# Layer 0 cross attention of a two-layer transformer: queries by seven block products for twelve of sixteen elements, the total of the sums formed earlier, and a weight folding of the second FFN moved

## The chip, the cores and the metric

The kernel runs on one core of a Trainium2 chip. The metric is the device time of one execution in microseconds (us). Three executions of the kernel before took 2147.99, 2148.72 and 2149.63 us; their median, 2148.72, is the time before. One further execution was profiled.

Engines are called as in the profile: PE multiplies matrices (PEld is its loading of the stationary operand), DVE, ACT and POOL are the vector, scalar and GpSimd engines, SP issues most DMAs. PE writes to PSUM, eight banks of 512 fp32 per partition; POOL reads and writes SBUF alone.

## The reference

Sixteen elements x[b] of 256 tokens by 256 features go through two layers, in fp32. Each layer is self attention, cross attention to a context of 256 tokens by 192 features, and an FFN, with residuals:

```
h = layernorm(x) * (1 + scale(cond)) + shift(cond)
q = h @ wq ; k, v = split(ctx_n @ wkv)          # layer 0: 16 heads of 64, rotary on q and k
x = x + softmax(q k^T / 8) v @ wo + bo
h2 = layernorm(x) ...                            # FFN: x = x + gelu(h2 @ w1 + b1) @ w2 + b2
```

In layer 0 wq is 256 x 1024, so the queries of one element are a 256 x 256 by 256 x 1024 product. The queries of the cross attention of layer 0 are what most of the change concerns. The second FFN is that of layer 1.

## The kernel before, in words

The work is a list of jobs: phase p (0: self of layer 0, 1: cross of layer 0, 2: FFN, 3 to 5: the same for layer 1) times element b. An attention job has two steps, s = 0 and 1, of two units each; a unit is four heads. The order of the instructions on each engine is the order of the code (a manual schedule); an instruction waits in its engine's queue until what it needs has happened, and whatever stands behind it waits too. A tile pool with a given number of buffers makes a writer wait for the last reader of the buffer that it takes over.

In step (b, s) of a layer 0 attention the code emits, for the probabilities of the units 2s and 2s + 1 (whose scores were formed at the end of the step before): on DVE the sum of the two halves of the probabilities (`stage_t`, tile both), its transposition in blocks (`stage_turn`, tile squares) and a reduction (`stage_reduce`, tile rows); on PE the products with the values (`layer0_sums`, L817), copied to SBUF by ACT (tile raw). In between it prepares the next step: queries and keys (`rotary`, `stage_rotary`). There PE forms q and k of one half unit side by side in one bank, DVE multiplies the bank by cosines and sines (tiles m, L707, 128 x 512), and POOL combines two such tiles (tile qk, L715, 128 x 512). At the end of the step PE forms the scores of the next step's two units (`scores`, `stage_s`, L750) in the eight banks, and ACT takes the exponential (L763).

Each product is cut in four strips of 32 output partitions that run side by side in the array (`product`, L84); one fp32 matmul shows as two records in the trace.

The tail of an element: when its four units are reduced, `sum_up` lets PE add the rows across partitions (the total), DVE takes the reciprocal, SP writes it to DRAM (sums_seen) and reads it back spread over 32 partitions each (tile spread), and POOL multiplies the four raw tiles by it (`scale`, L806). POOL then forms sums of blocks (`fold_inner`, L1099: 5, 2, 1 in step 0 and 7, 6 in step 1), and PE multiplies them by folded blocks of wo, seven products in place of eight (`finish_folded`), after which DVE adds them to x. In the kernel before, all of this for element b - 1 lies in element b's steps: the total in step 0 after the first rotations, the products at the end of step 1.

In step 0 PE also forms the values of the next element (`layer0_values`), and DVE the moments of the element three ahead and of its context; in step 1 DVE normalizes both, SP turns them through DRAM (turned, fetched), and ACT and POOL apply the modulation (tile hT).

The self phase (p = 0) already forms queries by seven block products for the elements 3 to 15: with wq and h cut into 2 x 2 blocks, seven products of sums of blocks take the place of eight products of blocks. `fold_query_weights` forms the sums of the weights once, `fold_tokens` those of h for each element (both on POOL), `query_part` issues the products in seven parts, with copies by ACT (tiles kept) and two additions by DVE on the way, `keys` forms the keys apart, and `rotate` turns queries and keys in separate tiles (L612 and L618 on DVE, L627 on POOL, 128 x 256 each on POOL).

In an FFN the elements from 2 on go in pairs (`pair_hidden`, again seven products). At the border between the elements 1 and 2 of layer 1's FFN, DVE folds the inputs of the pair (`fold_input`, L935 to L938), then the blocks of w2 (`fold_output_weights`, L1009 to L1012), then takes moments, and then adds the first of pair_hidden's sums (L968), which PE waits for before it may write that bank again.

## Time and profile before

| | us |
|---|---|
| median of three executions | 2148.72 |
| profiled execution, timed | 2152.08 |
| its span in the profile | 2150.3 |
| PE busy | 2136.8 |
| DVE busy | 1676.3 |
| POOL busy | 1340.8 |
| ACT busy | 905.9 |
| one cross element of layer 0 (809 to 847 us) | 38.42 |
| one self element of layer 0 with queries by seven (334 to 374 us) | 39.66 |

A timeline row reads: start and duration in us, engine, line, operation, output<-inputs, shapes, how many instructions were merged, and in brackets the time that the engine stood idle before it and what ended that. A row of the table by stretches gives the length, then the busy time of PE, weight loads, DVE, ACT and POOL (in parentheses how many instructions), then the clock granted to PE as a share of full speed, the share of DMA and GB/s.

### The profile page before, as it was taken

Reading aid. Unit: us, or ns where it says so; the run is one execution under the profiler, and the core shown is the slowest. Engines: PE = TensorE matmul, PEld = TensorE weight load, DVE = VectorE, ACT = ScalarE, POOL = GpSimd, SP = SyncE. Lnnn points to the kernel's source line nnn. Section 1 sums busy time; section 2 is a strip of 40 time slices with the busy share of each in tenths; the row PEclk is TensorE's granted clock in tenths of the full one; section 3 lists DMA queues with packets and bytes.
Section 4 is the critical chain, followed back from the end, with each engine's and each line's share of the span. In section 5 each row is a group of like instructions: output and inputs, shape, how many; then the busy total and the mean of one; then the engine's idle time right before and its main releaser. Section 6 shows DMA issues by size and latency. Waiting matters only on the chain.

```text
span 2150.3 us, 112524 instructions
## 1 busy us (share of the span) xinstructions
PE 2136.8 (99%) x51248; PEld 1442.3 (67%) x51248; DVE 1676.3 (78%) x3060; ACT 905.9 (42%) x1455; POOL 1340.8 (62%) x1346
## 2 busy tenths in 40 slices
PE   9999999999999999999999999999999999999998
PEld 5666767767766666666666658886666655656887
DVE  5878888888888888888888867865777777777765
ACT  3333334333342333333333334433666666664442
POOL 4888778778768777776777756662322233235773
PEclk9999999999999999999999999999999999999999
DMA  6110110110132311212212033221212232223321
GB/s 196 29 39 23 29 38 23 29 38 23 40 109 59 90 45 39 63 35 48 55 41 58 23 80 88 56 49 23 63 39 43 51 98 62 61 49 78 76 64 40
DMA packets 307039, 117.83 MB, mean 55 GB/s; under 512 B 243364, under 2 KB 289784, under 8 KB 306424
## 3 DMA queue, kind: packets, MB, share of 16 engines
q1 hardware_dynamic: 305320, 108.71, 20.7%
q8 instruction: 403, 6.60, 1.3%
q10 hardware_dynamic: 1232, 1.84, 0.3%
q14 instruction: 84, 0.69, 0.1%
HBM read 77.14 MB, written 33.29 MB: 51 GB/s over the span
## 4 chain that ended last, share of the span: by engine, by line
PE 85%; DVE 3%; POOL 3%; issue 1%; DMA 1%; SPq 0%; ACT 0%; DVEq 0%; POOLq 0%; ACTq 0%
PE banks L84 54%; PE banks L750 15%; PE banks L817 9%; PE banks L836 5%; PE banks L686 2%; PE banks L503 1%; POOL raw L806 1%; POOL folded L1099 1%; POOL qk L627 0%; DMA spread<-sums_seen 0%; POOL qk L715 0%; DVE x L1053 0%; DVE bn L351 0%; POOL rstd L357 0%; SPq L797 0%
## 5 line engine op out<-in xcount | busy, mean ns | idle before, releaser
L763 ACT ACTIVATE pr<-banks 128x1024 f32<-128x1024 f32 x576 | 487.4, 937 | 434.1 <-PE banks L750 319.9
L715 POOL TENSOR_TENSOR qk<-m,m 128x512 f32<-128x512 f32 x152 | 221.4, 1478 | 123.8 <-DVE m L707 119.0
L769 DVE TENSOR_TENSOR both<-pr 128x1024 f32<-128x1024 f32 x128 | 177.8, 1389 | 86.1 <-ACT pr L763 84.6
L750 PE MATMUL banks<-qk 32*64 32x256 f32 x8192 | 240.9, 378 | 1.0 <-POOL qk L715 0.5
L817 PE MATMUL banks<-pr,v 128*32 128x256 f32 x4096 | 241.2, 379 | 0.0
L750 PEld LDWEIGHTS banks<-qk 32*64 32x64 f32 x8192 | 184.7, 131 | 61.3 <-issue 16.8
L827 ACT COPY raw<-banks 128x512 f32<-128x512 f32 x128 | 75.1, 587 | 331.4 <-PE banks L817 327.5
L707 DVE TENSOR_TENSOR m<-banks,rope 128x512 f32<-128x512 f32 x304 | 189.7, 679 | 22.5 <-POOL qk L715 13.4
L627 POOL TENSOR_TENSOR qk<-m,m 128x256 f32<-128x256 f32 x208 | 168.0, 832 | 61.9 <-DVE m L618 38.6
L817 PEld LDWEIGHTS banks<-pr,v 128*32 128x32 f32 x4096 | 132.4, 110 | 94.1 <-issue 17.3
L806 POOL TENSOR_TENSOR raw<-raw,spread 128x512 f32<-128x512 f32 x128 | 162.1, 1296 | 22.9 <-DMA spread<-sums_seen 22.5
L453 POOL TENSOR_TENSOR x<-x,bo_b 128x256 f32<-128x256 f32 x96 | 73.3, 783 | 162.5 <-DVE xh L365 162.5
L878 POOL TENSOR_TENSOR oT<-oT,spread 128x256 f32<-128x256 f32 x64 | 45.8, 736 | 205.2 <-DVE spread L877 205.2
L775 DVE STREAM_TRANSPOSE squares<-both 128x1024 f32<-128x1024 f32 x128 | 158.0, 1235 | 1.8
L782 DVE TENSOR_REDUCE rows<-squares 128x32 f32<-128x1024 f32 x128 | 155.0, 1211 | 1.3
L1099 POOL TENSOR_TENSOR folded<-raw,raw 128x512 f32<-128x512 f32 x90 | 141.5, 1600 | 2.4
L836 PE MATMUL banks<-pr,wide_v 128*32 128x256 f32 x2048 | 134.3, 379 | 0.0
L84 PE MATMUL banks<-hT,wq_ca 128*32 128x256 f32 x2048 | 134.0, 379 | 0.0
L750 PE MATMUL banks<-q,k 32*64 32x256 f32 x4096 | 128.2, 381 | 0.0
L84 PE MATMUL banks<-hT,wk_sa 128*32 128x256 f32 x2048 | 126.5, 382 | 0.0
L1053 DVE TENSOR_TENSOR x<-banks,x 128x256 f32<-128x256 f32 (+2 forms) x150 | 79.6, 531 | 56.1 <-PE banks L84 49.8
L750 PEld LDWEIGHTS banks<-q,k 32*64 32x64 f32 x4096 | 87.4, 131 | 38.0 <-issue 13.9
(270 smaller groups left out, 4408.9 us busy)
## 6 DMA issues: line engine op xcount, KB each, us to landing
turned<-blocks SPq DMA_DIRECT2D x380, 64.0 KB
fetched<-turned SPq DMA_DIRECT2D x380, 64.0 KB
spread<-sums_seen SPq DMA_DIRECT2D x128, 128.0 KB
x<-in_x SPq DMA_DIRECT2D x16, 256.0 KB
fetched_c<-turned_c SPq DMA_DIRECT2D x64, 64.0 KB
cT<-in_ctx_turned SPq DMA_DIRECT2D x16, 256.0 KB
out<-x SPq DMA_DIRECT2D x15, 256.0 KB
ctx<-in_ctx SPq DMA_DIRECT2D x16, 192.0 KB
```

Source lines behind the costliest of these rows:

```text
L84: nc.tensor.matmul(out[cut], lhsT[:, cut], rhs, start=start, stop=stop, **more)
L627: nc.gpsimd.tensor_tensor(out, cos[i], sin[1 - i], (ALU.subtract, ALU.add)[i])
L707: nc.vector.tensor_tensor(m, pq, rope[:, s : s + 1, :].to_broadcast([P, 2, N]), ALU.mult)
L715: nc.gpsimd.tensor_tensor(r, x, y, (ALU.subtract, ALU.add)[out])
L750: nc.tensor.matmul(banks[64 * g : 64 * g + 64, at + h, t * N : (t + 1) * N], lhs, rhs, start=(half == 0 and (t == 0 or job["layer"] == 1)) ...
L763: nc.scalar.activation(pr[:, one], sc[:, one], AF.Exp, scale=0.125 if job["layer"] == 0 else 0.25)
L769: nc.vector.tensor_tensor(both, pr[:, :, 0, :], pr[:, :, 1, :], ALU.add)
L775: nc.vector.transpose(job["squares"].rearrange("p b k -> p (b k)"), job.pop("both").rearrange("p h n -> p (h n)"))
L806: nc.gpsimd.tensor_tensor(part, part, spread[:, u : u + 1, :].to_broadcast([P, 2, N]), ALU.mult)
L817: nc.tensor.matmul(o[32 * h : 32 * h + 32, half, :], v[:, t, col : col + 32], pr[:, h, t, :], start=(t == 0), stop=(t == NT - 1),)
L836: nc.tensor.matmul(o[32 * h : 32 * h + 32], v[:, t, 4 * c + h, 32 * e : 32 * e + 32], pr[:, h, t, :], start=(t == 0), stop=(t == NT - 1),)
L1099: eng.tensor_tensor(folded[m], *sums[m])
```

## The change

1. Cross phase of layer 0, elements 4 to 15: the queries are formed by seven block products, as in the self phase. The weights' sums are formed in step 1 of the elements 2 and 3, on POOL; the sums of h in step 0 of the element before, on POOL, one of them in place in hT. The keys' rotations come before the queries'. The banks differ: keys in the banks 0 and 1, queries in 2 and 3.
2. For these elements the total of the sums is formed in `finish_folded` of step 1, before the last of its seven products, in place of the following step 0. The write and the spread read are issued there too, ahead of the turned blocks. In step 0 POOL scales the first raw tile ahead of the rotations, the second after the keys' rotations, the others after the queries'.
3. Layer 1's FFN: `fold_output_weights` on DVE moves from step 3 of element 1 to step 0 of element 2, behind pair_hidden's first sum.
4. Small tiles share pools (flat with ctx, its turned blocks with blocks), bn has two buffers in place of four and inv32 one in place of two.

The diff, cut:

```diff
     def fold_tokens(job, eng):
         b = [[job["hT"][:, k, t * P : (t + 1) * P] for t in range(NT)] for k in range(KC)]
+        if job["cross"]:
+            few = work.tile([P, 3, P], F32, tag="tokens", name=f"tokens_{job['key']}", bufs=1)
+            t1, (t2, t3, t4) = b[0][1], (few[:, i] for i in range(3))
+            eng.tensor_tensor(t3, b[1][1], b[0][1], ALU.subtract)
+            eng.tensor_tensor(t1, b[0][1], b[0][0], ALU.subtract)
+            eng.tensor_tensor(t2, b[1][1], t1, ALU.subtract)
+            eng.tensor_tensor(t4, b[1][0], t2, ALU.subtract)
...
     def queries_by_seven(then):
-        return then is not None and then[0]["p"] == 0 and then[0]["b"] > 2
+        return then is not None and then[0]["layer"] == 0 and then[0]["b"] > (3 if then[0]["cross"] else 2)
...
+    def form_total(job, at):
+        product(bank(at, 32), job.pop("rows").rearrange("p u b -> p (u b)"), fold, True, True)
...
-    def finish_folded(job, at, between=None):
+    def finish_folded(job, at, between=None, total=None):
...
             for c in range(4):
                 product(places[m], hidden[m][:, c, :], weights[m][:, c, :], c == 0, c == 3)
+            if m == 7 and total:
+                form_total(total, 6)
...
+        if total:
+            sum_up(total, 6)
         nc.vector.tensor_tensor(outer, third[:, 0:1, :].to_broadcast([P, 2, P]), outer, ALU.add)
...
-            if b == 2 and s == 0 and layer0:
-                add()
+            if b == 2 and s == 0:
+                if layer0:
+                    add()
+                else:
+                    fold_output_weights(job["phase"], nc.vector)
...
                     fold_input(jobs[j + 1 : j + 3], nc.vector)
-                    if not layer0:
-                        fold_output_weights(job["phase"], nc.vector)
...
-            if queries_by_seven(then):
+            if queries_by_seven(then) and then[0]["cross"]:
+                early = s == 0 and "spread" in late
+                stage_t(job, 2 * s)
+                stage_turn(job, 2 * s)
+                for half in range(2):
+                    keys(then, 0, half)
+                query_part(then, 0)
+                for half in range(2):
+                    keys(then, 1, half)
+                stage_t(job, 2 * s + 1)
+                if early:
+                    scale(late, 0)
+                elif s == 0:
+                    sum_up(late, 6)
+                rotate(then, 0, 1)
+                if s == 1:
+                    fold_inner(late, nc.gpsimd, 7, 6)
+                rotate(then, 1, 1)
+                if early:
+                    scale(late, 1)
+                query_part(then, 1)
+                query_part(then, 2)
+                layer0_sums(job, 2 * s, 4, (0,))
+                query_part(then, 3)
+                layer0_sums(job, 2 * s, 4, (1,))
+                query_part(then, 4)
+                stage_reduce(job, 2 * s)
+                if s == 1:
+                    stage_turn(job, 3)
+                layer0_sums(job, 2 * s + 1, 5)
+                query_part(then, 5)
+                if s == 0 and queries_by_seven((nxt, 0)):
+                    fold_tokens(nxt, nc.gpsimd)
+                rotate(then, 0, 0)
+                query_part(then, 6)
+                rotate(then, 1, 0)
+                if s == 0:
+                    scale(late, *((2, 3) if early else range(4)))
+                    stage_turn(job, 1)
...
+                stage_reduce(job, 2 * s + 1)
+            elif queries_by_seven(then):
...
-                if then:
+                if then and then[0]["cross"]:
+                    finish_folded(late, (4, 5), total=job if queries_by_seven(then) else None)
+                elif then:
                     finish_folded(late, (4, 5), (lambda: stage_reduce(job, 3)) if queries_by_seven(then) else None)
```

## The prediction

> **What bounds the kernel now.** I read the page's busy times, then the idle times of each engine over the span, then the order of time of one cross element of layer 0, and last the same for a self element, which already forms its queries by seven block products.
>
> ```profile
> span 2150.3 us, 112524 instructions
> ...
> PE 2136.8 (99%) x51248; PEld 1442.3 (67%) x51248; DVE 1676.3 (78%) x3060; ACT 905.9 (42%) x1455; POOL 1340.8 (62%) x1346
> ```
>
> ```profile
> 814.95:833.78 18.83, 18.83 (x364) 10.00 (x360) 18.47 (x34) 5.68 (x8) 10.88 (x11) 1.00 0.37 88
> 833.78:853.37 19.59, 19.59 (x533) 14.55 (x529) 14.41 (x21) 7.26 (x11) 17.59 (x14) 1.00 0.04 10
> ```
>
> These two stretches are the halves (step 0, step 1) of one cross element, each from the start of its scores; after the span come PE, weight loads, DVE, ACT, POOL. PE has no gap: 18.83 + 19.59 = 38.42 us, and the following elements repeat it to 0.1 us. Time goes only if matmul work goes. DVE is next, 32.9 of 38.4 us.
>
> ```profile
> 820.09 1.05 PE L84 MATMUL banks<-hT,wq_ca 128*32 128x256 f32 x16
> 820.96 0.61 PE L84 MATMUL banks<-cT,wk_ca 128*32 128x256 f32 x8
> ```
>
> ```profile
> 366.48 0.62 PE L84 MATMUL banks<-hT,wq_sa 128*32 128x128 f32 x16
> 366.92 0.62 PE L84 MATMUL banks<-tokens,wq_sa 128*32 128x128 f32 x16
> 367.35 1.91 PE L84 MATMUL banks<-hT,wk_sa 128*32 128x256 f32 x32
> ```
>
> Starts count, not the durations, which overlap. 16 records of 256 columns, a quarter of a step's queries, take 0.87 us. A block product (16 records of 128 columns) takes 0.44, 0.43: half, so the shorter stream costs nothing extra.
>
> ```profile
> 1960.22 1.05 PE L84 MATMUL banks<-hT,w_b 128*32 128x256 f32 x16
> 1963.35 1.07 PE L84 MATMUL banks<-inner,input_w_L_xcond_b 128*32 128x256 f32 x16 [2.09 <-DVE sums L968]
> 1964.24 3.37 PE L84 MATMUL banks<-w_b,g 128*32 128x128 f32 x64
> ...
> 1978.07 1.93 PE L84 MATMUL banks<-w_b,g 128*32 128x128 f32 x64
> ```
>
> ```profile
> 1961.20:1963.40 2.20, 0.11 (x8) 0.05 (x7) 2.06 (x7) 0.84 (x2) 0.56 (x1) 1.00 0.40 90
> 1963.40:1965.50 2.10, 2.10 (x48) 1.76 (x52) 1.92 (x5) 1.05 (x2) 1.57 (x3) 0.77 0.81 219
> 1965.50:1967.40 1.90, 1.90 (x43) 1.90 (x39) 0.76 (x2) 0.96 (x3) 1.82 (x3) 0.50 1.00 372
> ```
>
> This is the longest PE wait of the kernel, in the second FFN: 2.09 us for DVE. After it the granted clock (the third figure from the end) falls to 0.77 and 0.50; 64 records that take 1.74 us later (1978.07 to 1979.81) take 3.12 (1964.24 to 1967.36).
>
> **Part 1: the queries.** Removed per step: four quarters of 0.865, 3.46 us. Added: seven block products of 16 records, 7 x 0.436 = 3.05 us. Gain 0.41 us a step; 12 elements x 2 steps: **-9.8 us**, if PE gets no new waits. The key products and what they wait for keep their number. The self phase shows that it need not: its elements take 39.66 us, PE busy 39.66. But the cross phase is fuller, so I lay out both steps, with T0 and T1 the starts of their scores. PE: 18.83 - 0.41 - 0.06 (the total moves) = 18.36 for step 0, 19.59 - 0.41 + 0.06 = 19.24 for step 1, together 37.60.
>
> ACT gains one copy within the bank and two "kept" copies (0.37 each): 2.2 us an element on an engine busy 12.9; PE needs each some 0.9 us after it is made. Nothing.
>
> DVE gains two adds of 0.42 a step, 1.7 us an element: 34.6 of 37.6. Its waits before show the room:
>
> ```profile
> 837.87 1.50 DVE L769 TENSOR_TENSOR both<-pr 128x1024 f32<-128x1024 f32 x1 [3.37 <-ACT pr L763]
> ```
>
> Step 1, from T1 + 4.1 (first exponentials done): two sums of probabilities with a transposition between 3.83, key rotations 2.40, add 0.42, reduction 1.2, transposition 1.25, both query rotations with the second add 2.87, reduction 1.15: T1 + 17.2. PE forms the total at T1 + 18.3, one product before the end: **1.1 us to spare**. This is the new wait; behind it on PE stands all that follows. Residual adds, reciprocal, norm and context norm then end by T0 + 3.9, when the next exponentials end at T0 + 4.1. Step 0 from T0 + 4.25: 7.7 us of the same work to T0 + 11.95, the query rotations (released by PE at 12.7) to 15.5, the rest to 20.8 = T1 + 2.4. In time.
>
> POOL turns each unit's two 512-wide rotations (2.52 us) into two pairs of 256-wide ones (2 x 1.43), +1.4 us an element, and gains four token sums: in the self rows 0.46, 1.42 (median), 0.46, 0.46, together 2.9 us with the gaps. Its order in step 0 is what matters: the first scaling now stands ahead of all rotations, and it waits for a DMA.
>
> ```profile
> 346.45 0.35 DVE L791 RECIPROCAL inv<-banks 128x32 f32<-128x32 f32 x1
> 354.52 2.53 POOL L806 TENSOR_TENSOR raw<-raw,spread 128x512 f32<-128x512 f32 x2 [0.28 <-DMA spread<-sums_seen]
> 1092.76 0.34 DVE L791 RECIPROCAL inv<-banks 128x32 f32<-128x32 f32 x1
> 1102.32 4.97 POOL L806 TENSOR_TENSOR raw<-raw,spread 128x512 f32<-128x512 f32 x4 [1.72 <-DMA spread<-sums_seen]
> ```
>
> ```profile
> 349.22 2.27 POOL L627 TENSOR_TENSOR qk<-m,m 128x256 f32<-128x256 f32 x2 [1.52 <-DVE m L618]
> 352.80 1.43 POOL L627 TENSOR_TENSOR qk<-m,m 128x256 f32<-128x256 f32 x2 [1.31 <-DVE m L618]
> ```
>
> From reciprocal to landing: 8.1 us (self), up to 9.6 (cross, behind the turned blocks and the context in SP's queue). The change puts sums and spread ahead of those, so I take 8.1. The reciprocal starts near T0 - 0.5: landing T0 + 7.6, scaling to 8.9, key pairs (DVE done at 9.1 and 10.3) to 12.0, scaling 13.2, tokens 16.1, query pairs 17.6 and 19.0. Scores want them at 18.36 and 20.2: **0.8 us to spare**; at 9.6 us latency 0.5 short (scaling to 10.4, and all behind it 1.3 later). On SP the turned writes wait for sums and spread, about 1.5 us later than now; their fetch was issued at T0 + 14.1 and is used at T1 + 14: hidden. The context follows them, at about T0 + 10 instead of 8.8, and is read at T0 + 18 or later: hidden. Tile renames and pool depths: DVE uses the moment tiles in order, nothing.
>
> The row for tokens was taken beside DVE's sums of probabilities. [...]
>
> The sums of the query weights (eight POOL adds of 0.83, two elements' step ends, a whole element before use): hidden; at elements 2 and 3 they could delay POOL once by 3 us, of which 0 to 1 shows. I take 0.3.
>
> **Part 2: second FFN.** Without four DVE sums (0.7, 0.6, 0.6, 0.6) the awaited sum ends at 1960.8 instead of 1963.3, before PE needs it (1961.09). PE gains 2.26 there. But the four now stand ahead of the norm (1.35) and of the next sum: 1960.8 + 2.5 + 1.35 + 0.65 = 1965.3, and PE, at full clock, comes to it at 1963.7: a new wait of 1.6 us. PE's product of 1967.36 starts at 1965.4: -2.0. With the clock up, the 0.29 that this product and the next lost to the half clock (1.16 for 0.87) is won too: -2.3. If the clock falls as it did after 2.09 us, 1.38 + 0.29 is lost again: -0.6. The nearer row is the wait of 2.09 (another, 0.52 at 1958.47, left the clock at 1.00), but the new one is shorter, so I take the middle, **-1.4**, and keep both ends.
>
> [...]
>
> **Sum.** -9.8 - 1.4 + 0.3, and 0.5 for two such waits of 0.25 us as scores have for POOL in the run before (1254.70: 0.28): -10.4 us. The profiled span goes from 2150.3 to 2139.9 (that execution was timed at 2152.08, 3.4 above the median); the median from 2148.72 to **2138.3**.
>
> **Rivals.** (a) Part of the gain is eaten: spread late as in the cross rows (9.6 us) or the total 0.4 us late costs 0.35 to 0.7 an element, 4 to 8 us: 2142.3 to 2146.3. For it: rooms of 0.8 and 1.1 us. Against: the shorter SP queue. (b) Slower: POOL is late in step 0. Each us behind shows once an element at the scores, and POOL's tail in step 1 then holds the rotation tiles, DVE's reduction and the total. The gain of 10.4 is gone at 0.87 us an element, and +0.2% is reached at 1.22; past the room of 0.8 that is POOL 1.7 and 2.0 us later than laid out, for instance 9.6 us latency (1.3) plus one stretched pair (0.84, the rows of 2.27 against 1.43). Some 2153 to 2160. (c) No change: weight loads, 128 columns apiece, become the limit and queries save nothing; only Part 2 remains, 2147.3. Against: 0.436 us a product in the self rows.
>
> **Chances.** Forecast (2135.5 to 2142) 0.66, (a) 0.16, (b) 0.11 slower and 0.03 around zero, (c) 0.04. The low end is -9.8 - 2.3 with no waits, less 1 us for the spread of runs; the range 2135.5 to 2146 holds the forecast and nearly all of (a), 0.81. A measurement tells 0.2% (4.3 us) from no change, at 2144.4, which splits (a) 0.09 to 0.07: faster 0.75, same 0.14, slower 0.11.
>
> **What would show it.** Right: cross elements 5 to 14 at 37.6 us with PE busy as long; query products of 0.436; PE waits on the POOL rotations and on the total under 0.2 us each; FFN wait of 2.09 gone, a shorter one some 2.5 us on. Wrong: PE or its weight loads waiting for the POOL query rotation at each step 1's scores, for the reduction ahead of the total, or the spread's DMA landing later than T0 + 8.5.

## The result and the profile after

The changed kernel takes 2143.04 us (median of 10 runs, 2141.77 to 2144.71); the kernel before, run beside it, 2148.60 (2144.99 to 2150.51). The ratio is 0.9975, with a 95% interval of 0.9965 to 0.9984: 5.6 us less. The forecast was 10.4 us less, 2138.3, with a range of 2135.5 to 2146. The direction is right and the time lies in the range, but about half of the gain is missing. Where it went is the subject of what follows.

The page of the changed kernel begins like that of before: PE is busy for 99% of the span.

```profile
span 2141.9 us, 115148 instructions
...
PE 2125.1 (99%) x52400; PEld 1472.1 (69%) x52400; DVE 1697.6 (79%) x3108; ACT 931.5 (43%) x1527; POOL 1375.6 (64%) x1498
```

The steady elements are as forecast. These are PE rows of the timeline of the changed kernel (start, time, engine, line, operation, out<-in, number of records): the scores of element 6's step 1 and of element 7's steps 0 and 1, with two of the block products in the first of these steps.

```profile
910.50 3.71 PE L768 MATMUL banks<-qk 32*64 32x256 f32 x128
...
922.55 0.62 PE L84 MATMUL banks<-tokens,wq_ca 128*32 128x128 f32 x16
922.99 0.62 PE L84 MATMUL banks<-hT,ms_of_query_weights_True 128*32 128x128 f32 x16
...
929.75 3.71 PE L768 MATMUL banks<-qk 32*64 32x256 f32 x128
...
948.10 3.71 PE L768 MATMUL banks<-qk 32*64 32x256 f32 x128
```

A block product starts 0.44 us after the one before it. The two steps take 19.25 and 18.35 us; the undisturbed elements take 37.56, where 38.42 stood before. That is 0.86 us an element, a little more than the 0.82 forecast.

The loss stands at the two ends of the run of elements. Here are the PE rows with the longest waits of that phase (the wait and its releaser in brackets), again of the changed kernel.

```profile
814.50 0.22 PE L84 MATMUL banks<-fold,rows 128*32 128x32 f32 x1 [0.99 <-DVE rows L800]
...
822.50 0.65 PE L84 MATMUL banks<-hT,wq_ca 128*32 128x128 f32 x16 [0.78 <-POOL wq_ca L559]
...
1245.98 0.66 PE L768 MATMUL banks<-qk 32*64 32x256 f32 x6 [1.83 <-POOL qk L643]
1246.91 5.38 PE L768 MATMUL banks<-qk 32*64 32x256 f32 x122 [0.27 <-DVE m L629]
```

The first two belong to elements 3 and 4, where the block products begin: PE waits for the total of the sums, which waits for DVE, and then for the sums of the query weights. The last two are the scores of element 15's step 1, for which POOL's rotations come late. They also take 5.4 us in place of 3.7. The windows from 1245.98 on say why: the third figure from the end is the granted clock.

```profile
1245.98:1247.98 2.00, 1.73 (x38) 1.08 (x46) 2.00 (x3) 0.00 (x0) 1.68 (x3) 0.91 0.68 251
1247.98:1249.98 2.00, 2.00 (x48) 1.59 (x40) 1.97 (x6) 0.01 (x1) 2.00 (x3) 0.50 0.14 44
1249.98:1251.98 2.00, 2.00 (x60) 1.43 (x46) 0.86 (x4) 1.93 (x2) 1.90 (x3) 0.73 0.04 8
```

In the second FFN the wait of 2.09 us is gone, and the new one stands 3 us later, ahead of the next product. It is 1.38 us long (1.6 were forecast), and the clock stays at 1.00.

```profile
1956.02 1.93 PE L84 MATMUL banks<-w_b,g 128*32 128x128 f32 x64
1959.33 1.07 PE L84 MATMUL banks<-inner,w_b 128*32 128x256 f32 x16 [1.38 <-DVE sums L1010]
```

One reading needs care. The two profiled spans differ by 8.4 us, the medians by 5.6. The profiled execution of before was one of the longer ones of its kernel, and the time from the start to element 3's scores, which the change leaves as it was and the later kernels nearly so, varies between 774.0 and 778.6 us over the thirteen profiles of this study. So the stages are compared one by one below, each by its own length.

### The profile page after: what moved, and what is told of

It is laid out like the page before. It is cut to its first block, busy times and chain, and to the rows that moved or that the text cites. A ratio compares the mean times of both kernels' runs of the same rounds, so it can differ in the third digit from the quotient of the medians.

```text
span 2141.9 us, 115148 instructions
## 1 busy us (share of the span) xinstructions
PE 2125.1 (99%) x52400; PEld 1472.1 (69%) x52400; DVE 1697.6 (79%) x3108; ACT 931.5 (43%) x1527; POOL 1375.6 (64%) x1498
## 3 DMA queue, kind: packets, MB, share of 16 engines
q10 hardware_dynamic: 1232, 1.84, 0.2%
## 4 chain that ended last, share of the span: by engine, by line
PE 85%; POOL 3%; DVE 3%; issue 1%; DMA 1%; SPq 0%; ACT 0%; DVEq 0%; POOLq 0%; ACTq 0%
PE banks L84 54%; PE banks L768 15%; PE banks L839 9%; PE banks L858 5%; PE banks L704 1%; PE banks L503 1%; POOL raw L828 1%; POOL folded L1121 1%; POOL qk L733 0%; DMA spread<-sums_seen 0%; DMA sums_seen<-inv 0%; DVE x L1075 0%; DVE m L629 0%; POOL qk L643 0%; DVE xh L365 0%
## 5 line engine op out<-in xcount | busy, mean ns | idle before, releaser
L643 POOL TENSOR_TENSOR qk<-m,m 128x256 f32<-128x256 f32 x400 | 303.9, 788 | 78.8 <-DVE m L636 47.2
L787 DVE TENSOR_TENSOR both<-pr 128x1024 f32<-128x1024 f32 x128 | 182.8, 1428 | 63.2 <-ACT pr L781 59.8
L828 POOL TENSOR_TENSOR raw<-raw,spread 128x512 f32<-128x512 f32 x128 | 168.5, 1337 | 50.8 <-DMA spread<-sums_seen 40.3
L629 DVE TENSOR_TENSOR m<-banks,rope 128x512 f32<-128x512 f32 x200 | 128.3, 683 | 21.7 <-PE banks L84 12.1
L636 DVE TENSOR_TENSOR m<-banks,rope 128x512 f32<-128x512 f32 x200 | 125.2, 676 | 1.7 <-POOL qk L643 0.8
L733 POOL TENSOR_TENSOR qk<-m,m 128x512 f32<-128x512 f32 x56 | 78.3, 1419 | 35.3 <-DVE m L725 32.4
```

What stands on the lines that cost most here:

```text
L629: nc.vector.tensor_tensor(view, bank(2 + e if job["cross"] else 2 * e).rearrange("p (t h n) -> p t h n", t=2, h=2), rope[:, i, :].rearrang ...
L643: nc.gpsimd.tensor_tensor(out, cos[i], sin[1 - i], (ALU.subtract, ALU.add)[i])
L787: nc.vector.tensor_tensor(both, pr[:, :, 0, :], pr[:, :, 1, :], ALU.add)
L828: nc.gpsimd.tensor_tensor(part, part, spread[:, u : u + 1, :].to_broadcast([P, 2, N]), ALU.mult)
```

## The experiments

### The kernel before, once more

Is the wait of 2.09 us with its fallen clock in every execution, or was the first profile an unlucky one?

> The kernel before, unchanged, profiled a second time. Theory A (the wait and the fallen clock in the second FFN belong to every execution): a PE wait of about 2.1 us for the DVE sums of the second FFN again, the granted clock at 0.77 and 0.50 after it, span near 2150. Theory B (the first profiled execution, timed 3.4 us above the median, was an unlucky one): the wait is 1 us or less, or the clock stays at 1.00 after it, and the span is 1.5 to 3.5 us shorter, 2146.5 to 2148.5. In both the steady cross elements take 38.4 us.

The wait is there again, 2.09 us to a hundredth, but the clock does not fall. These are the PE rows and two windows behind them.

```profile
1963.55 1.07 PE L84 MATMUL banks<-inner,input_w_L_xcond_b 128*32 128x256 f32 x16 [2.09 <-DVE sums L968]
1964.44 1.93 PE L84 MATMUL banks<-w_b,g 128*32 128x128 f32 x64
```

```profile
1964.60:1965.60 1.00, 1.00 (x48) 1.00 (x40) 1.00 (x3) 0.45 (x1) 1.00 (x2) 1.00 0.72 139
1965.60:1966.60 1.00, 1.00 (x37) 0.85 (x32) 0.85 (x2) 0.72 (x3) 1.00 (x2) 1.00 1.03 426
```

The 64 records take 1.93 us here; in the first profile of before they took 3.37. Each theory was right in one half: the wait belongs to the kernel, the clock does not. The span was 2150.1, no shorter, because of waits elsewhere (1.46 us for POOL at 601 us, in a stretch that the change does not touch).

### The second FFN alone

```diff
 (the kernel before)
-            if b == 2 and s == 0 and layer0:
-                add()
+            if b == 2 and s == 0:
+                if layer0:
+                    add()
+                else:
+                    fold_output_weights(job["phase"], nc.vector)
...
                     fold_input(jobs[j + 1 : j + 3], nc.vector)
-                    if not layer0:
-                        fold_output_weights(job["phase"], nc.vector)
```

> The kernel before with the second FFN's four weight sums moved, and nothing else. Theory A: the whole of what the two profiles show there, 2.1 + 0.3 us, so 2.2 to 2.6 us faster than before by the medians (2146.2 of 2148.6). Theory B: what is won is the shorter wait alone, or less, 0 to 1 us (2147.6 to 2148.6). The profile is to show the wait of 2.09 gone, one of 1.2 to 1.6 us for the later DVE sums about 1 us before the output products, and a clock of 1.00 there, by both.

Measured: 2147.90 against 2148.80 of before, ratio 0.9996 (0.9988 to 1.0005), that is 2.6 us less to 1.1 more. By the medians alone nothing can be said. The stretch itself is clearer. From the hidden products ahead of the wait to the last output products of the pair it takes 17.71, 16.37 and 16.31 us in the three profiles without the move (the first with the fallen clock), and 14.20 to 14.82, in the mean 14.47, in the ten with it. So the move is worth 1.9 us against the two profiles in which the 64 records behind the wait took 1.93 us, the clock up, and 3.2 against the one in which the clock fell to 0.50 and they took 3.37. The new wait was 0.98 us in this run and 1.04 to 1.38 in the others (mean of the ten 1.22). Two smaller waits are gone as well: one of 0.52 us for DVE ahead of the long one in the first profile, and one of 0.65 and 0.56 us behind it, for which the profile names no releaser, in the other two.

### The queries alone

```diff
 (the changed kernel)
-            if b == 2 and s == 0:
-                if layer0:
-                    add()
-                else:
-                    fold_output_weights(job["phase"], nc.vector)
+            if b == 2 and s == 0 and layer0:
+                add()
...
                     fold_input(jobs[j + 1 : j + 3], nc.vector)
+                    if not layer0:
+                        fold_output_weights(job["phase"], nc.vector)
```

> The changed kernel without the move in the second FFN: queries and total only. By both theories the steady elements take 37.56 us and the waits at the entry (elements 3 and 4) and at the last element stand as in the changed kernel. Theory A: 3.0 to 3.5 us faster than before by the medians (2145.3), that is the whole 5.6 less the FFN's 2.3. Theory B: 4.6 to 5.6 us faster (2143.0 to 2144.0).

Measured: 2143.53 against 2148.80, ratio 0.9979 (0.9969 to 0.9988), 5.3 us less, as the second theory had it, though the interval (2.6 to 6.7 us) holds the first as well. The profile repeats the waits of the changed kernel: 0.98 for the rows, 0.79 for the weight sums, 1.84 ahead of the last scores. This time the clock stayed up after the 1.84: the 122 records of those scores took 3.69 us, in place of 5.38.

With these profiles the queries' part can be read without the noise of the rest: from the scores of element 3's step 1 to those of element 15's step 1 the kernels with direct queries take 456.1, 455.8 and 456.1 us, those with block products 451.2, 451.4 and (in a later run) 452.1. At 37.56 an element without a wait it would be 445.4 (19.21 for element 3's step 1, eleven elements of 37.56, and 13.52 less 0.48 for the last step). So of 10.6 us, 4 to 5 arrive.

### Three edits at the two ends

```diff
 (the changed kernel)
-            if s == 1 and job["b"] in ((2, 3) if job["cross"] else (1, 2)):
-                weights_after = job["b"] - 2 if job["cross"] else job["b"] - 1
+            if job["cross"] and (job["b"], s) in ((2, 1), (3, 0)):
+                weights_after = job["b"] - 2
...
-        if layer0 and not ffn and s == 1 and job["b"] == 3:
+        if layer0 and not ffn and s == (0 if job["cross"] else 1) and job["b"] == 3:
             late_mod = phases[job["p"] + 1]
...
-                layer0_sums(job, 2 * s + 1, 5)
+                if not leaving:
+                    layer0_sums(job, 2 * s + 1, 5)
                 query_part(then, 5)
...
                 rotate(then, 1, 0)
+                if leaving:
+                    layer0_sums(job, 1, 5)
                 if s == 0:
-                    scale(late, *((2, 3) if early else range(4)))
+                    scale(late, *((1, 2, 3) if leaving else (2, 3) if early else range(4)))
...
```

> The changed kernel with three edits: the second half's weight sums formed one step sooner, the FFN's factors computed one step sooner (both at element 3), and in element 15's step 0 the last sums over values placed after the query products, with the second scaling after the query rotations. My theory: the queries' gain is lost at the two ends of the run of elements, 2.5 us at the entry and 3.0 to 3.4 at the last element. Then the waits there (0.99 for the DVE rows, 0.78 and 0.28 for the weight sums, 1.83 and 0.27 before the last scores) shrink below 0.3 each, the clock stays at 1.00 at the last scores, and the time is 4 to 5.5 us below the changed kernel's 2143.0, at 2137.5 to 2139. Rival: the waits are DVE's and POOL's load of work that has to be done anyway; they come up again a step later, and the time is within 1 us of 2143.0.

A miss: 2145.51 against 2148.80, ratio 0.9986 (0.9977 to 0.9994), less of a gain than the changed kernel's. The last element was mended: its step 0 took 13.77 us in place of 14.94, the wait of 1.83 was 0.32, and the clock stayed up: the 122 records of the scores took 3.69 us. But element 3's step 1 took 27.01 us in place of 20.78. The second half's weight sums, moved to the end of step 0, stand ahead of step 1's rotations on POOL. These are rows of POOL, DVE and PE from that step.

```profile
809.95 0.73 POOL L561 TENSOR_TENSOR ms_of_query_weights_True<-wq_ca,ms_of_query_weights_True 128x256 f32<-128x256 f32 x1
810.63 1.40 POOL L643 TENSOR_TENSOR qk<-m,m 128x256 f32<-128x256 f32 x2
```

```profile
812.07 1.29 DVE L629 TENSOR_TENSOR m<-banks,rope 128x512 f32<-128x512 f32 x2 [4.35 <-POOL qk L643]
...
815.89 1.29 DVE L629 TENSOR_TENSOR m<-banks,rope 128x512 f32<-128x512 f32 x2 [2.19 <-POOL qk L643]
817.10 1.21 DVE L800 TENSOR_REDUCE rows<-squares 128x32 f32<-128x1024 f32 x1
```

```profile
818.36 0.26 PE L84 MATMUL banks<-fold,rows 128*32 128x32 f32 x1 [3.91 <-DVE rows L800]
```

The chain reads upward: PE waits for the rows; DVE forms them right after its last query rotation; that rotation waited because the tiles `m`, two of each kind, were not free; POOL frees them when it has added the key rotations, and POOL was late. So 3.2 us of POOL work (four sums, 807.51 to 810.68) at the end of a step 0 cost 6.2 us against the changed kernel's first profile, and 5.2 against the kernel further below that leaves these sums in step 1 (21.79). This gave a new theory: the loss at the entry comes through these buffers, not through DVE's own work.

### The changed kernel again

> The changed kernel, unchanged, timed beside the others of this set. Both theories: 2141.5 to 2144.5 by the median; from the scores of element 3's step 1 to those of element 15's step 1 451.2 us (451.2 and 451.4 in the two profiles so far, against 456.1, 455.8 and 456.1 with the old queries). My theory of the clock, that after a wait of 1.8 to 2.1 us it falls in some executions and not in others: the wait of 1.83 before the last scores is there again, and the scores take 3.7 us (clock up) or 5.4 (clock down), either way.

2142.39 against 2148.93, ratio 0.9974 (0.9963 to 0.9985). The stretch takes 452.1 us. The wait for the rows at element 3 is 2.23 us here (0.99 in the first profile): DVE waited 2.24 us for POOL's buffers, against 1.13. The scores after the wait of 1.83 took 5.38 us, as in the first profile, with the clock down again.

### The three places, mended with less

The weight sums stay in step 1, only ahead of the norm and the inputs of later elements; the other two edits (the factors, and element 15's last sums and scaling) are as above.

```diff
 (the changed kernel, with the factors and element 15 as above)
             else:
+                if weights_after is not None and job["cross"]:
+                    fold_query_weights(job["phase"], weights_after, nc.gpsimd)
                 prepare_norm(third)
                 prepare_context(third)
...
```

> As the kernel with all three edits, but the second half's weight sums stay at the end of step 1 of element 3 and only go ahead of the norm and the input of later elements there; the factors one step sooner and the last sums after the query products as in that kernel. My theory: the 6.2 us that kernel lost at element 3 came from 3.3 us of POOL work standing ahead of step 1's rotations; here POOL idles at that place for DVE (3.1 us in that kernel's profile). From the scores of element 3's step 1 to those of element 15's step 1: 451.2 less 0.99 (total), less 0.8 to 1.06 (weight sums), less 1.1 (last element): 448.0 to 448.4; the time 2 to 4.5 us below the changed kernel beside it. Rival (the losses at the ends are paid wherever that work stands): 450.5 or more, within 1 us of it.

2139.63 (2138.70 to 2140.94) against 2142.39 of the changed kernel beside it (2140.29 to 2147.39); ratio to before 0.9960 (0.9946 to 0.9973). The waits for the weight sums are gone (element 4's step 0 takes 18.35), and the last step takes 13.77. But the wait for the rows is 2.25 us although DVE was spared the factors: the stretch is 450.0, not the 448.0 to 448.4 expected. DVE's own load is not what delays the total: in the second profile of the changed kernel too the factors took 0.19 us each in place of 1.20, and the wait was the longer one. These are POOL's and DVE's rows at that place.

```profile
794.89 5.98 POOL L828 TENSOR_TENSOR raw<-raw,spread 128x512 f32<-128x512 f32 x4
800.95 4.76 POOL L1121 TENSOR_TENSOR folded<-raw,raw 128x512 f32<-128x512 f32 x3
```

```profile
812.34 1.29 DVE L629 TENSOR_TENSOR m<-banks,rope 128x512 f32<-128x512 f32 x2 [2.26 <-POOL qk L643]
813.54 1.21 DVE L800 TENSOR_REDUCE rows<-squares 128x32 f32<-128x1024 f32 x1
```

Element 3's step 0 is the last with direct queries. There the total is still formed in step 0, so the four scalings stand behind all rotations, and the four token differences, new in that step, stand ahead of them. POOL carries its lateness into step 1. The profiles at hand order themselves by it. Where POOL's key rotations begin 11.9 us after the scores of element 3's step 1 (the changed kernel's first profile, the queries alone), PE waits 0.98 or 0.99 us for the rows; where they begin 12.9 us after them (its second profile and this kernel), 2.23 or 2.25.

### The total back in its place

If that is so, then the other part of the change, the total half an element sooner, which the prediction priced at nothing, is what keeps POOL's scalings out of the way in every element.

```diff
 (the changed kernel)
-                    finish_folded(late, (4, 5), total=job if queries_by_seven(then) else None)
+                    finish_folded(late, (4, 5))
```

> The changed kernel with the total of the sums formed half an element later again, in step 0 behind the key products, as before the change; the query products stay. Theory A, the prediction's pricing of that part at nothing: steady elements 37.56 +- 0.1 and only the wait of 0.99 for the DVE rows at element 3 gone, 1 us shorter in all or the same. Rival: the earlier total is what lets the queries pay: the spread lands near T0 + 15 instead of T0 + 7, POOL's four scalings and the folds behind them go past the end of step 0, step 1's rotations come late, and each element costs 0.5 to 1.5 us more (38.1 to 39.1).

Most elements take 38.16 to 38.39 us, 0.6 to 0.8 more than 37.56, and the stretch takes 457.4: more than with direct queries (456.0). Of the elements 5 to 14 two lie outside: element 9 takes 39.41, element 14 37.56. The rival was right. Without the earlier total at most 0.26 of the 0.86 us an element is left, and over the stretch the block products win nothing. All four of POOL's scalings now stand behind the query rotations, 18.4 us after the scores of step 0 (element 7, scores at 933.72), and the folds behind them end 10.0 us into step 1 (7.3 in the changed kernel):

```profile
952.08 4.99 POOL L828 TENSOR_TENSOR raw<-raw,spread 128x512 f32<-128x512 f32 x4
957.15 5.62 POOL L1121 TENSOR_TENSOR folded<-raw,raw 128x512 f32<-128x512 f32 x3
```

In the elements 5 to 14 the only PE waits of a quarter of a microsecond or more are two, both at element 9 and both for DVE's residual adds (0.64 and 0.31). Elsewhere the loss is in the scores of step 0, which take some 4.3 us in place of 3.71, behind the same chain.

```profile
969.39 1.29 DVE L629 TENSOR_TENSOR m<-banks,rope 128x512 f32<-128x512 f32 x2 [1.12 <-POOL qk L643]
970.59 1.21 DVE L800 TENSOR_REDUCE rows<-squares 128x32 f32<-128x1024 f32 x1
971.72 0.41 DVE L1137 TENSOR_TENSOR x<-x,banks 128x256 f32<-128x256 f32 x1
```

```profile
971.91 4.33 PE L768 MATMUL banks<-qk 32*64 32x256 f32 x128
```

The rotation waits for POOL, the reduction and the residual adds stand behind it on DVE, and the adds have to read the banks that the scores overwrite. This kernel was profiled once (2149.86 us).

### A ladder of POOL work, and where it bites

The prediction named 0.8 us of room on POOL ahead of the query rotations of step 0. The 1.8 in the text below is that room with 1.9 us for the four token rows in place of 2.9, as the trace of the changed kernel has them (0.46 us each). This kernel adds useless repeats of two token differences there (1.07 us a pair), from none up to four pairs.

```diff
 (the changed kernel)
                     fold_tokens(nxt, nc.gpsimd)
+                    made = nxt["tokens"]
+                    for _ in range(max(0, (job["b"] - 5) // 2)):
+                        nc.gpsimd.tensor_tensor(made[6], made[3], made[5], ALU.subtract)
+                        nc.gpsimd.tensor_tensor(made[4], made[2], made[6], ALU.subtract)
                 rotate(then, 0, 0)
```

> The changed kernel with useless repeats of two token differences on POOL in step 0, ahead of the query rotations: none at elements 4 to 6, then 1, 2, 3 and 4 pairs at elements 7 and 8, 9 and 10, 11 and 12, 13 and 14; a pair is 2 x 0.46 and two gaps, 1.07 us. It measures the room that the prediction put at 0.8 us (1.8 with the shorter tokens). By the 0.8: 37.8 at one pair, 38.9 at two, 39.9 at three, 41.0 at four. By the trace of the changed kernel, where tokens take 1.9 instead of 2.9 and the spread lands about 1 us sooner than laid out (room 2.5 to 2.8): 37.56 at one and two pairs, 38.0 at three, 39.1 at four. The slower case of the prediction: more than 1 us lost for each us of POOL once the room is gone, since POOL's lateness holds DVE's total in step 1 too.

The same ladder was run once more, later, with the last reduction of step 1 placed ahead of DVE's last query rotation, so that the total no longer stands behind POOL's buffers.

```diff
 (the ladder)
                 query_part(then, 6)
+                if s == 1:
+                    stage_reduce(job, 3)
                 rotate(then, 1, 0)
...
-                stage_reduce(job, 2 * s + 1)
+                if s == 0:
+                    stage_reduce(job, 1)
```

> The ladder of useless POOL work again (1, 2, 3, 4 pairs of 1.07 us at elements 7 to 14), on the changed kernel with the reduction ahead of the last query rotation in step 1. In the first ladder one pair cost 0.5 to 0.95 us an element, two 1.25, three 2.3, four 3.7 to 4.2. If the cost comes through the reduction that stands behind the rotation: one pair 0 to 0.2, two 0.2 to 0.6, three 1.0 to 1.7 (the wait at step 1's scores, 1.1, stays). Rival (POOL's order paces the step whatever stands behind it): the same costs as in the first ladder within 0.3.

The times from one element's scores to the next one's, in us:

| pairs added (elements) | ladder | ladder, reduction first |
|---|---|---|
| 0 (5, 6) | 37.56, 37.75 | 37.56, 37.56 |
| 1 (7, 8) | 38.51, 38.04 | 37.57, 37.65 |
| 2 (9, 10) | 38.87, 38.78 | 37.96, 38.55 |
| 3 (11, 12) | 39.85, 39.82 | 38.76, 38.77 |
| 4 (13, 14) | 41.72, 41.25 | 41.52, 41.50 |

In the first ladder there is next to no room: the first 1.07 us costs 0.5 to 0.95 (0.95 at element 7, where POOL's first scaling could begin only 9.0 us after the scores, 0.5 at element 8 with 7.5), and a wait of 0.6 us for the rows appears with it (at element 7), while the scores of step 1, where the prediction looked for it, wait for POOL only from three pairs on (1.12 us). At two pairs the chain stands in the rows of DVE and PE:

```profile
1040.00 1.29 DVE L629 TENSOR_TENSOR m<-banks,rope 128x512 f32<-128x512 f32 x2 [1.11 <-POOL qk L643]
1041.21 1.21 DVE L800 TENSOR_REDUCE rows<-squares 128x32 f32<-128x1024 f32 x1
```

```profile
1042.47 0.22 PE L84 MATMUL banks<-fold,rows 128*32 128x32 f32 x1 [0.60 <-DVE rows L800]
```

With the reduction first, one pair is free, two cost 0.4 to 1.0, three 1.2. That is one edit on DVE, with POOL's work unchanged, and it gives back about a microsecond of room: the order on DVE was the link. At four pairs both cost the same 3.9: there the scores wait 1.9 to 2.2 us, the clock falls to 0.50, and the scores take 5.4 to 5.7 in place of 3.71.

### The entry, by its cause

Two kernels try the theory at the entry, both on top of the three mended places. The first forms element 2's total early as well and puts element 3's scalings between the rotations:

```diff
 (the kernel with three mended places)
-                    finish_folded(late, (4, 5), total=job if queries_by_seven(then) else None)
+                    finish_folded(late, (4, 5), total=job if then[0]["b"] > 2 else None)
...
+                if summed:
+                    scale(late, 0, 1)
                 rotary(then, 0, 0)
                 rotary(then, 0, 1)
+                if summed:
+                    scale(late, 2)
...
-                if late is not None and s == 0:
+                if late is not None and s == 0 and not summed:
                     sum_up(late, 6)
...
```

> The kernel with three mended places, and the total of element 2's sums formed early as well (in step 1 of element 2), so that at element 3's step 0, the last with direct queries, the scalings stand between the rotations on POOL and not all behind them. My theory of the entry loss: POOL leaves step 0 of element 3 late (four scalings, 6.0 us, and the folds behind the rotations), so in step 1 the key rotations come late, DVE's last query rotation waits for their buffers (2.26 us in that kernel's profile), and the reduction that the total needs stands behind it on DVE. Then the PE wait for the rows at element 3 goes from 2.25 to under 0.3, that step from 21.8 to 19.2 to 19.7 us, and the stretch from element 3's step 1 to element 15's step 1 from 450.0 to 447.5 to 448.5; time 1 to 2.5 us less, a ratio to before of 0.995. Rival (DVE's own work is too much there): the wait stays at 0.8 or more, the stretch above 449.

The second only puts the reduction ahead of the rotation, as in the second ladder:

> The kernel with three mended places, and in step 1 of the elements with block products the last reduction of the sums placed ahead of the last query rotation on DVE. If the reduction is late only because it stands behind a rotation that waits for POOL's buffers, the wait for the rows at element 3 (2.25) goes. The rotation is then 1.2 us later, which the next scores may feel: at element 3 they wait for POOL in its stead, the step takes 20.3 to 21.3 (21.8 before), and steady elements keep 37.56 to 37.7. Rival: the rotations are needed at once everywhere and each element gets 0.3 to 1.2 us longer.

The first takes 2138.08 us (2135.59 to 2139.65) against 2148.65, ratio 0.9957 (0.9943 to 0.9970). Element 3's step 1 takes 19.21 us and element 4's step 0 18.35, the steady values: nothing is lost at the entry any more. The stretch takes 447.2 us. POOL now has scalings between the rotations of step 0, and in step 1 DVE's rotation and reduction follow each other without a wait:

```profile
781.69 2.53 POOL L828 TENSOR_TENSOR raw<-raw,spread 128x512 f32<-128x512 f32 x2 [3.14 <-DMA spread<-sums_seen]
...
787.76 1.29 POOL L828 TENSOR_TENSOR raw<-raw,spread 128x512 f32<-128x512 f32 x1
...
793.77 1.28 POOL L828 TENSOR_TENSOR raw<-raw,spread 128x512 f32<-128x512 f32 x1
```

```profile
808.08 1.29 DVE L629 TENSOR_TENSOR m<-banks,rope 128x512 f32<-128x512 f32 x2
809.29 1.21 DVE L800 TENSOR_REDUCE rows<-squares 128x32 f32<-128x1024 f32 x1
```

The second takes 2137.93 us (2137.25 to 2140.35), ratio 0.9956 (0.9942 to 0.9969). Element 3's step 1 takes 19.26 us, better than expected (20.3 to 21.3), but element 4's step 0 then takes 19.81: the two together 39.07, where the kernel with three mended places has 40.14 and the first of these two 37.56. So the order on DVE alone gives back 1.1 of the 2.6 us. POOL is as late in that kernel as without the edit: its key rotations begin 12.9 us after the scores of element 3's step 1, against 9.6 in the first of the two. Steady elements stay at 37.56. Both beat the changed kernel and the one before by their medians; against the changed kernel they were not timed side by side, and the intervals of their ratios overlap its interval a little.

## Why the prediction was half right

**The queries, -9.8 us: right in the steady state.** Each element is 0.86 us shorter, 10.3 in twelve, with PE full and block products of 0.44 us. That alone sets rival (c), queries that save nothing, aside.

**The range: met in part by luck.** 2143.04 lies where rival (a) was placed (2142.3 to 2146.3), but (a) had the loss in every element, through a late spread or a late total. Measured, the elements between keep nearly all of their gain, and the loss stands at the entry and at element 15, which no rival priced at that size.

**Entry, +0.3 us: wrong, 3 to 4.** The prediction asked whether the weight sums could delay POOL once. It priced neither the transition element, whose step 0 still has the old order on POOL and four token differences besides, nor the use of the second half's weight sums right after they are made: it had them "a whole element before use", but PE waits 0.78 and 0.28 us for those made in step 1 of element 3. Measured are 1.5 to 2.5 us through the total (20.7 to 21.7 in place of 19.21) and 1.5 through the weight sums (19.83 in place of 18.35). With the causes removed both go to zero.

**Element 15: counted as a gain of 0.41 us, in truth a loss.** The prediction took all 24 steps as alike. In the last step 0 no next element's values stand between the query products and the scores, and the sums over values, which there covered the direct queries' rotations (3.64 us of PE), have been moved ahead of the last block products. These are PE's rows ahead of those scores, before and in the changed kernel:

```profile
1247.91 3.64 PE L817 MATMUL banks<-pr,v 128*32 128x256 f32 x64
1251.48 2.94 PE L750 MATMUL banks<-qk 32*64 32x256 f32 x80
```

```profile
1240.50 2.77 PE L839 MATMUL banks<-pr,v 128*32 128x256 f32 x48
...
1243.53 0.62 PE L84 MATMUL banks<-hT,ms_of_query_weights_True 128*32 128x128 f32 x16
```

The scores then wait 1.83 us for POOL. Against a step that has its share of the gain this is 1.9 us, and where the clock falls after the wait (to 0.50) the scores lose another 1.7 (in three of the six profiles that have this wait). With these sums and one scaling behind the query products the step takes 13.77 us in place of 14.94.

**The total, priced at nothing: wrong in kind.** The prediction treated it as a new wait with 1.1 us of room. That wait stays away in the steady elements. But the part earns 0.6 to 0.8 us an element by bringing POOL's scalings forward; without it the queries' gain is eaten.

**Rooms.** 1.1 us ahead of the total and 0.8 at the scores were laid out as two separate rooms. They are one chain. The layout of step 1 let the rotations run as DVE reached them; it left out that their tiles come free only when POOL has added the key rotations. POOL's lateness hence reaches the total first, and less than 1 us of it is free. The rival of a late POOL had the link ("POOL's tail in step 1 then holds the rotation tiles, DVE's reduction and the total") but put it behind the room at the scores. Its price, about 1 us of time for each us of POOL beyond the room, is near what the ladder shows (0.5 from one pair to two, 0.95 from two to three), up to the rung where the clock falls. In the steady state the kernel did not go that way because the tokens took 2.0 us, not 2.9: the query pairs end 16.7 to 17.3 and 18.1 to 18.7 us after T0 in the elements 5 to 14 (17.6 and 19.0 laid out). The spread had no part in that. POOL's first scaling began 6.4 to 7.0 us after the reciprocal in seven of these elements and 8.6 to 8.8 in three (8.1 taken), but in six of the seven it then took 2.0 to 2.4 us, beside DVE's sum of probabilities, and the key pairs ended at T0 + 12.0 to 12.6 in all ten (12.0 laid out). Here is POOL in element 7 (T0 = 929.75), the first scaling and the query pairs:

```profile
936.69 2.33 POOL L828 TENSOR_TENSOR raw<-raw,spread 128x512 f32<-128x512 f32 x1 [2.49 <-DMA spread<-sums_seen]
...
945.29 2.79 POOL L643 TENSOR_TENSOR qk<-m,m 128x256 f32<-128x256 f32 x4
```

The 2.9 us for the tokens were read from the self phase, where the second of the four rows takes 1.42 us in the median, beside DVE's sum of probabilities (0.46 in the two of 14 elements where that sum stood elsewhere). In the new place no such sum stood beside the four rows, and each of them took 0.46 to 0.47 us in all twelve elements.

**Second FFN, -1.4 us between -0.6 and -2.3: undersized.** The clock stayed up after each of the ten new waits of 0.98 to 1.38 us (granted in the first profile after: 1.00). The term is -1.9 us against executions of before with the clock up, -3.2 against one where it fell. The forecast started from the latter, where its case of a clock that stays up gave -2.3. The rest is the new wait (1.2 us, 1.6 forecast) and the wait of 0.52 at 1958.47, which it left standing and which is gone. Its own run could not show it in the medians.

**The sum** over the stretch, for the first profile after: -10.6 for the steady gain (the last step with it), +1.6 and +1.5 at the entry, +1.9 at the last element, 0.8 in the elements 5 to 14 beyond 37.56 each (0.5 taken; 0.55 of it in element 9, where the scores of step 0 take 4.1 us), together -4.8, as 456.0 to 451.2 has it. With the FFN's 1.9 (clock up) that makes 6.7, and 8.0 beside an execution of before whose clock fell there. The two timings of the changed kernel gave 5.6 us (3.4 to 7.5) and 6.5 (3.2 to 8.0); what lies between these and 6.7 is within the spread of the untouched stages and was not followed further.

## What to carry to other kernels

A gain per element holds for the elements that look alike; lay out the first and the last one by themselves, with what stands in front of them in the old order and what no longer follows them. When an instruction is laid out on an engine, ask for its destination buffer as well as its inputs: an engine with room to spare sets the pace of another through the buffers that it frees (here POOL, busy for 64% of the span, for which DVE's last query rotation of element 3 waited 1.13 and 2.24 us in two profiles). An edit that seems to be only preparation may carry the gain; undo it alone before it is priced at nothing.

## What was not expected of the hardware

The granted clock falls after some PE waits and not after others of the same length. Over the thirteen profiles, 20 waits of 0.9 to 1.5 us (those of the first 100 us aside) never brought it down. Of 15 waits of 1.83 to 2.25 us, eight did (to 0.50) and seven did not: the same wait of 2.09 us at the same place fell once in three, that of 1.83 three times in six. In the run of all three edits it fell in the course of a wait of 3.91 us that had one of 2.40 us just ahead of it, and the scores behind it took 5.01 us in place of 3.71. No profile here shows what decides it. So in this kernel a saved wait of 2 us is worth more than itself: after eight of 15, the slow stretch behind it goes as well (1.7 us at the last scores, 1.3 in the second FFN).

DVE instructions of 0.19 us took the time of a POOL instruction when POOL was at work. These are the FFN's factors in the first profile of the changed kernel, beside POOL's four scalings (794.60, 5.01 us together, 1.25 each), and then in the kernel with the early entry, where POOL was idle (it waited for the spread until 781.69):

```profile
795.98 1.20 DVE L178 SCALAR_TENSOR_TENSOR add_a<-add_a,cols 128x32 f32<-128x32 f32 x1
797.21 1.20 DVE L179 TENSOR_TENSOR add_a<-add_a,cols 128x32 f32<-128x32 f32 x1
```

```profile
778.85 0.19 DVE L178 SCALAR_TENSOR_TENSOR add_a<-add_a,cols 128x32 f32<-128x32 f32 x1
779.08 0.19 DVE L179 TENSOR_TENSOR add_a<-add_a,cols 128x32 f32<-128x32 f32 x1
```

Six times the time, for 32 elements a partition. Over the thirteen profiles all 55 such rows (L177 to L180, without those that read a bank, which took 0.19 us in the profiles of before and after, beside POOL or not) with POOL idle took 0.19 us. Of 153 beside a POOL instruction 149 took 0.61 to 1.32, the shortest of them, 0.61 and 0.67, beside two of 0.7 to 0.8, and the four of 0.19 began within 0.02 us of POOL's own. So in this kernel such instructions are to be counted at 0.6 to 1.3 us beside a busy POOL.
